# Softmax attention of three of four groups of sequences placed beside the first six units of a gated delta rule

## The chip, the cores and the metric

The kernel runs on one core of a Trainium2 chip, in 32-bit floats. The core's engines are TensorE (PE, matrix products; its weight loads are listed apart as PEld), VectorE (DVE), ScalarE (ACT), GpSimd (POOL) and SyncE (SP, which here only issues DMA transfers). Each engine works through its own instructions in order, and semaphores make it wait for others. A scheduler below the program decides the final order of each engine from the order in which the program issues its steps and from what depends on what.

The metric is the device time of one execution in microseconds (us). Where a time of the kernel is given it is the median of several executions; the profile is of one execution.

## The reference

Sixteen sequences of 128 tokens, 256 wide, pass through two residual blocks:

```python
x = x + delta_rule(attention(x, cond, Wq, Wk, Wv, Wo), W_qkv, W_z, W_b, W_a, conv_w, dt_bias, A_log, norm_w, W_out)
x = x + quantized_ffn(lora_ffn(x, ..., adapter_of_sequence), ...)
```

The attention is causal softmax attention with 16 heads of 16, its queries scaled by `min(precision, 4)` of the sequence; its result h feeds the delta rule:

```python
mixed = silu(causal_conv(h @ W_qkv, conv_w))        # 4 taps; 16 q and k heads, 32 v heads, 128 wide
q, k, v = split(mixed)
beta = sigmoid(h @ W_b)
g = -exp(A_log) * softplus(h @ W_a + dt_bias)
core = chunk_gated_delta_rule(l2norm(q), l2norm(k), v, g, beta)   # chunks of 64
core = core * rsqrt(mean(core * core) + 1e-6) * norm_w * silu(h @ W_z)
return core @ W_out
```

In the chunked rule g is summed along each chunk, its differences give a decay matrix, and a triangular system of 64 by 64 is solved for every head and chunk. The second block is a feed-forward network with an adapter per sequence, and a second one with weights rounded to 8-bit floats.

## The kernel before

The sequences are in four groups of four (`NG`, `GS`); a group has 512 tokens (`GT`). Four stages follow each other.

**1. Attention** (L119 to about L320, in pools `w1`, `p1` and its own three PSUM pools `ps_a`, `ps_s`, `ps_t`). `project(g)` makes queries, keys and values of a group; keys are copied twice (`ke`), each with the heads of one parity set to zero. The loop over n has NB + 2 slots; in a slot three sequences are worked on, at different steps: `scores(n)` (products `ps_sc` at L200, scale and mask into `sc` on DVE at L206, maximum at L212 on DVE, subtraction at L215 on POOL), `soften(n-1)` (exp on ACT at L229, sum at L234 and reciprocal at L235 on DVE, multiplication at L238 on POOL) and `weigh(n-2)` (transposes `ps_pt` L253 and copies, product with values `ps_o` L262, and a pick of the right head of each pair on ACT and DVE, L267 and L268). Each list has hand-written times that put the steps of a slot into one order. After four sequences `output(g)` multiplies by Wo and gives h of the group (`hT`, `ps_h` at L280) and the products for the gates (`ps_ba`).

**2. Gates**, `gates()` at L384, once for all sixteen sequences, when attention is done: `logs` (sigmoid, softplus by abs, exp and ln, on ACT and DVE), `rows` (sums along the chunk, stored in DRAM as `sums`) and `offsets`. SP then loads the sums of two units at a time, broadcast over partitions, into `aT` (`load_sums`, L427 on), and `fades` turns them into decay factors: a subtraction and a triangular select on POOL (L438, L439) and exp on ACT (L443).

**3. Units** of the delta rule, in pools `c2`, `w2`, `pc` and PSUM `ps_b` (six buffers) and `ps_r` (one, four accumulators of `ps_out`), which are opened after attention's have been closed. A unit is one key head with its two value heads for one group; there are 64. The loop `for n in range(N + LAST)` is a software pipeline with one slot for each unit, ordered by hand-written times between 0 and 24. In slot n:

- `keys` of unit n: products `ps_in` (L450), the first tap on ACT (L459), three taps on DVE (L461), silu (L478), squares (L482), norms (`ps_n`, L488; transposed on DVE, L490), factors on POOL (`nn`, L495, and `kn`, `c`);
- `decays` of unit n-1: weighting on POOL, products `ps_kq` (L525) and their scaling on DVE (L529), and DMAs that collect diagonal blocks (`diag`);
- for four units at a time (`NU`), `inverse`: 32 by 32 triangular inverses, mostly on DVE (products at L573), in two slots (units 0 to 3: slots 5 and 6), ending with `Tc` and `Uc`;
- `mergers` of unit n-7 (`MERGE`): DMAs that place `Uc` and `Tc` into the tiles `W` and `T`, and products that make 64 by 64 inverses of them. The first product is `ps_lo` at L664, in slot 7;
- `values` of unit n-7 (with weights `w_v`), `outputs` of unit n-8 (`w_gate`, `ps_z`, `ps_y`, `ps_ot`, norm) and `finish_unit` of unit n-10 (transposes `ps_zt`, `zT`, `ps_out` at L795, after the last head of a group the addition of x at L800 and the store of `x1`).

**4. Feed-forward networks**, in pools `w3` and `p3`, opened when the units' pools are closed. SP loads `acc` (all of x1, one transfer a group, L898), the adapter numbers and the weights, among them `gq`, `uq` and `dq`; `quantize` (L923 to L930) rounds these on DVE and POOL. PE transposes `acc` (`ps_xt`, L951), makes the adapter's small products (`lg`, `lu`, masked on DVE) and then `ps_gu` (L965), of which DVE makes `hid` (L974).

Of the kernel before, what the change touches and what calls it, by code (L numbers as in the profile page):

```python
# [53 lines left out]
def tile_adaln_attn_ffn(  # L54
# [16 lines left out]

    def filled(shape, value, name):
        t = const.tile(shape, F32, name=name, tag=name)
        G.memset(t, value)
        return t
# [3 lines left out]

    tri = pa.tile([P, P], F32, name="tri", tag="gm")  # L80
    G.memset(tri, 1.0)
    G.affine_select(out=tri, in_=tri, pattern=[[1, P]], compare_op=ALU.is_ge,
                    fill=0.0, base=0, channel_multiplier=-1)
    G.memset(tri[HALVES[0], HALVES[1]], 0.0)
    tri_2 = pa.tile([P, P], F32, name="tri_2", tag="gm2")
    G.tensor_copy(tri_2, tri)
    G.memset(tri_2[HALVES[0], HALVES[0]], -1.0)
    G.affine_select(out=tri_2[HALVES[0], HALVES[0]], in_=tri_2[HALVES[0], HALVES[0]], pattern=[[-1, C]],
                    compare_op=ALU.is_gt, fill=0.0, base=0, channel_multiplier=1)
# [6 lines left out]
    row = const.tile([P, 1], I32, name="row")  # L96
    G.iota(row, pattern=[[0, 1]], base=0, channel_multiplier=1)
    V.tensor_scalar(row, row, 4, 1, ALU.arith_shift_right, ALU.bitwise_and)
    odd = const.tile([P, 1], F32, name="odd")
    V.tensor_copy(odd, row)  # L100
    even = const.tile([P, 1], F32, name="even")
    V.tensor_scalar(even, odd, -1.0, 1.0, ALU.mult, ALU.add)
    parity = (even, odd)
# [7 lines left out]
    sums = dram.tile([NK * NB * 2, S], F32, name="sums")  # L111
# [3 lines left out]
    with ExitStack() as st:  # L115
        w1 = st.enter_context(tc.tile_pool(name="w1", bufs=1))
        p1 = st.enter_context(tc.tile_pool(name="p1", bufs=2))
        ps_a = st.enter_context(tc.tile_pool(name="ps_a", bufs=2, space=PSUM))
        ps_s = st.enter_context(tc.tile_pool(name="ps_s", bufs=4, space=PSUM))  # L119
        ps_t = st.enter_context(tc.tile_pool(name="ps_t", bufs=2, space=PSUM))  # L120

        xT_sb = w1.tile([P, ND, NT], F32, name="xT_sb")
# [9 lines left out]
        xTv = xT.rearrange("(c p) t -> p c t", p=P)  # L132
        for w, t in ((wqT, wq_sb), (wkT, wk_sb)):
            nc.sync.dma_start(out=t, in_=w.rearrange("(c p) e -> p c e", p=P))
        nc.sync.dma_start(out=xT_sb[:, :, 0:GT], in_=xTv[:, :, 0:GT])
        nc.sync.dma_start(out=wv_sb, in_=wvT.rearrange("(c p) e -> p c e", p=P))
        nc.scalar.dma_start(out=pr, in_=prec.rearrange("b o -> (b o)").partition_broadcast(P))
        nc.sync.dma_start(out=wo_sb, in_=woT.rearrange("(c p) e -> p c e", p=P))
        for g in range(1, NG):
            nc.sync.dma_start(out=xT_sb[:, :, g * GT : (g + 1) * GT], in_=xTv[:, :, g * GT : (g + 1) * GT])  # L140
# [6 lines left out]
        V.tensor_scalar(pr, pr, 4.0, 0.25, ALU.min, ALU.mult)  # L147

        grp = {}

        def project(g):
            d = grp[g] = {}
            qT = d["q"] = p1.tile([P, ND, GT], F32, name="qT", tag="qT")
            ke = d["k"] = p1.tile([P, ND, GS, 2, S], F32, name="ke", tag="ke")
            vt = d["v"] = p1.tile([P, GS, D], F32, name="vt", tag="vt")
            d["oT"] = p1.tile([P, ND, GT], F32, name="oT", tag="oT")

            def qk(w, e):
                ps = ps_a.tile([P, GT], F32, name="ps_qk", tag="a")
                for c in range(ND):  # L160
                    T.matmul(ps, lhsT=w[:, c, e * P : (e + 1) * P], rhs=xT_sb[:, c, g * GT : (g + 1) * GT],
                             start=c == 0, stop=c == ND - 1)
                if w is wq_sb:
                    A.copy(qT[:, e, :], ps)
                else:

                    for h in range(2):
                        A.activation(ke[:, e, :, h, :], ps.rearrange("p (s t) -> p s t", t=S), AF.Copy, scale=parity[h])

            def vproj(i):  # L170
                ps = ps_a.tile([P, 2, D], F32, name="ps_v", tag="a")
                for j in range(2):
                    t0 = g * GT + (2 * i + j) * S
                    for c in range(ND):
                        T.matmul(ps[:, j, :], lhsT=xT_sb[:, c, t0 : t0 + S], rhs=wv_sb[:, c, :],
                                 start=c == 0, stop=c == ND - 1)
                A.copy(vt[:, 2 * i : 2 * i + 2, :], ps)

            return (
                [lambda e=e: qk(wq_sb, e) for e in range(ND)]  # L180
                + [lambda e=e: qk(wk_sb, e) for e in range(ND)]
                + [lambda i=i: vproj(i) for i in range(GS // 2)]
            )

        HB = P // HD
        NPR = HB // 2
        seq = {}

        def scores(b):

            g, i = divmod(b, GS)
            d = seq[b] = {}
            cols = slice(i * S, (i + 1) * S)

            def product():

                d["ps"] = [ps_s.tile([P, ND, 2, S], F32, name="ps_sc", tag="s") for _ in range(NPR)]
                for e in range(ND):
                    for r in range(NPR):
                        T.matmul(d["ps"][r][:, e], lhsT=grp[g]["q"][BLOCKS[r], e, cols],  # L200
                                 rhs=grp[g]["k"][BLOCKS[r], e, i], start=True, stop=True)
                d["s"] = p1.tile([P, NPR, ND, 2, S], F32, name="sc", tag="sc", bufs=3)
                d["mx"] = p1.tile([P, 2, HB], F32, name="mx", tag="mx")

            def mask(r):
                V.scalar_tensor_tensor(out=d["s"][:, r].rearrange("p e h t -> p (e h) t"),  # L206
                                       in0=d["ps"][r].rearrange("p e h t -> p (e h) t"), scalar=pr[:, b : b + 1],
                                       in1=causal[:, None, :].to_broadcast([P, 2 * ND, S]),
                                       op0=ALU.mult, op1=ALU.add)

            def largest(n):
                V.tensor_reduce(out=d["mx"][:, n, :], in_=half(d, n), axis=AX.X, op=ALU.max)  # L212

            def less(n):
                G.tensor_tensor(half(d, n), half(d, n), d["mx"][:, n, :][:, :, None].to_broadcast([P, HB, S]),  # L215
                                ALU.subtract)

            return ([product] + [lambda r=r: mask(r) for r in range(NPR)]
                    + [lambda n=n, f=f: f(n) for n in range(2) for f in (largest, less)])

        def half(d, n):
            return d["s"][:, 2 * n : 2 * n + 2].rearrange("p r e h t -> p (r e h) t")

        def soften(b):

            d = seq[b]

            def exp(n):
                A.activation(half(d, n), half(d, n), AF.Exp)  # L229

            def total(n):
                if n == 0:
                    d["sm"] = p1.tile([P, 2, HB], F32, name="sm", tag="sm")
                V.tensor_reduce(out=d["sm"][:, n, :], in_=half(d, n), axis=AX.X, op=ALU.add)  # L234
                V.reciprocal(d["sm"][:, n, :], d["sm"][:, n, :])  # L235

            def share(n):
                G.tensor_tensor(half(d, n), half(d, n), d["sm"][:, n, :][:, :, None].to_broadcast([P, HB, S]), ALU.mult)  # L238

            return [lambda n=n, f=f: f(n) for n in range(2) for f in (exp, total, share)]  # L240

        def weigh(b):

            g, i = divmod(b, GS)
            d = seq[b]

            def turn(r):
                if r == 0:
                    d["pT"] = p1.tile([P, NPR, ND, 2, S], F32, name="pT", tag="pT")
                ps = ps_t.tile([P, ND, 2, S], F32, name="ps_pt", tag="t")  # L250
                for e in range(ND):
                    for h in range(2):
                        T.transpose(ps[:, e, h, :], d["s"][:, r, e, h, :], ident)  # L253
                A.copy(d["pT"][:, r], ps)

            def product(e):

                if e == 0:
                    d["po"] = ps_a.tile([P, ND, 2, S], F32, name="ps_o", tag="a")
                for r in range(NPR):  # L260
                    c0 = e * P + r * BL
                    T.matmul(d["po"][BLOCKS[r], e], lhsT=grp[g]["v"][:, i, c0 : c0 + BL],  # L262
                             rhs=d["pT"][:, r, e], start=True, stop=True)
# [9 lines left out]
        def output(g):  # L273
# [10 lines left out]
            def gates():  # L284
# [6 lines left out]
                if g > 1:  # L291
                    nc.sync.dma_start(out=h_dram[g], in_=hTs[g])
# [539 lines left out]
    for n in range(N + LAST):  # L832
# [47 lines left out]
        if n == N + 2:  # L880
            ffn_loads()
# [222 lines left out]
```

## Time and profile before

| what | us |
|---|---|
| time, median of 3 executions | 2496.53 |
| their range | 2491.33 to 2499.64 |
| the profiled execution's own time | 2490.03 |
| span of the profile (first to last instruction) | 2488.3 |
| first matrix product | 8.24 |
| first `ps_sc` | 21.84 |
| last `ps_o` of attention | 208.7 |
| first `ps_in` of unit 0 | 219.93 |
| first `ps_lo` (slot 7) | 354.79 |
| last `ps_out` of the units | 2059.55 |

The mean clock that TensorE was granted was 0.945 of full speed. All times below are from the start of the span. "Busy" is time in which an engine executes at least one instruction; a group's mean is that of one instruction, so that overlapping instructions (four `ps_sc` products run beside each other on different rows of the array) have a larger sum of means than busy time. The idle time at the end of a group's line is that of the engine just before these instructions, with the instruction whose end released it.

DMA issues that the text refers to, with KB of each and the median us from issue to landing:

```profile
aT<-sums SPq DMA_DIRECT2D x64, 512.0 KB, 5.3
w_qk<-in_w_qkv_dram SPq DMA_DIRECT2D x128, 128.0 KB, 2.3
w_v<-in_w_qkv_dram SPq DMA_DIRECT2D x64, 256.0 KB, 2.8
```

### The profile page before, as it was taken

Reading aid. Unit: us, or ns where it says so; the run is one execution under the profiler, and the core shown is the slowest. Engines: PE = TensorE matmul, PEld = TensorE weight load, DVE = VectorE, ACT = ScalarE, POOL = GpSimd, SP = SyncE. Lnnn points to the kernel's source line nnn. Section 1 sums busy time; section 2 is a strip of 40 time slices with the busy share of each in tenths; the row PEclk is TensorE's granted clock in tenths of the full one; section 3 lists DMA queues with packets and bytes.
Section 4 is the critical chain, followed back from the end, with each engine's and each line's share of the span. In section 5 each row is a group of like instructions: output and inputs, shape, how many; then the busy total and the mean of one; then the engine's idle time right before and its main releaser. Section 6 shows DMA issues by size and latency. Waiting matters only on the chain. (4 is left out here: it accounts for less than half of the span.)

```text
span 2488.3 us, 42071 instructions
## 1 busy us (share of the span) xinstructions
PE 2240.2 (90%) x16380; PEld 1488.2 (60%) x16380; DVE 1535.3 (62%) x2048; ACT 1330.4 (53%) x2954; POOL 1126.2 (45%) x813
## 2 busy tenths in 40 slices
PE   7996449899999899999989899999989997899999
PEld 4453226666676676666667676676767783344545
DVE  5663488687776968677696867769696522211111
ACT  4444326766666676766667676666766660011010
POOL 5664535465555646555564655456463224200000
PEclk9888679999999999999999999999999999999999
DMA  1004112222223322222332222233223213000000
GB/s 53 1 9 135 33 31 62 71 63 72 67 69 94 83 74 64 73 67 69 87 91 71 66 73 63 68 78 96 71 58 86 70 31 114 0 5 5 9 0 18
DMA packets 290533, 146.15 MB, mean 59 GB/s; under 512 B 183968, under 2 KB 279328, under 8 KB 290336
## 3 DMA queue, kind: packets, MB, share of 16 engines
q1 hardware_dynamic: 289904, 143.41, 21.7%
q8 instruction: 132, 2.16, 0.4%
q14 instruction: 65, 0.53, 0.1%
q10 hardware_dynamic: 432, 0.04, 0.0%
HBM read 116.91 MB, written 5.51 MB: 49 GB/s over the span
## 5 line engine op out<-in xcount | busy, mean ns | idle before, releaser
L461 DVE SCALAR_TENSOR_TENSOR cv<-ps_in,cw,cv 128x508 f32<-128x508 f32 (+2 forms) x768 | 539.7, 734 | 109.3 <-ACT cv L459 104.6
L459 ACT ACTIVATE cv<-ps_in,cw 128x512 f32<-128x512 f32 x256 | 174.4, 682 | 215.5 <-PE ps_in L450 214.1
L450 PE MATMUL ps_in<-hT,w_v 128*128 128x512 f32 x512 | 281.6, 678 | 5.8 <-DVE z L765 3.5
L450 PE MATMUL ps_in<-hT,w_qk 128*128 128x512 f32 x512 | 261.2, 635 | 11.2 <-DVE z L765 6.5
L765 DVE TENSOR_TENSOR z<-ps_ot,z 128x512 f32<-128x512 f32 x128 | 87.8, 686 | 290.1 <-ACT sq L763 290.1
L738 PE MATMUL ps_z<-w_gate,hT 128*128 128x256 f32 x1024 | 242.3, 379 | 0.8 <-DVE z L765 0.8
L795 PE MATMUL ps_out<-wo_head,zT 128*128 128x256 f32 x1024 | 239.6, 386 | 1.8 <-ACT zT L787 1.0
L495 POOL TENSOR_SCALAR nn<-turned 128x4 f32<-128x4 f32 x64 | 15.5, 242 | 469.2 <-DVE turned L490 342.0
L795 PEld LDWEIGHTS ps_out<-wo_head,zT 128*128 128x128 f32 x1024 | 188.7, 190 | 39.1 <-issue 12.0
L738 PEld LDWEIGHTS ps_z<-w_gate,hT 128*128 128x128 f32 x1024 | 189.5, 190 | 26.8 <-DVE z L765 1.7
L450 PEld LDWEIGHTS ps_in<-hT,w_v 128*128 128x128 f32 x512 | 102.9, 213 | 112.1 <-issue 105.4
L1026 POOL TENSOR_TENSOR o<-o,acc 128x512 f32<-128x512 f32 x8 | 10.1, 1264 | 337.0 <-DVE o L1025 337.0
L478 ACT ACTIVATE kq<-cv 128x512 f32<-128x512 f32 x128 | 80.1, 626 | 153.2 <-DVE cv L461 153.1
L763 ACT ACTIVATE sq<-ps_ot 128x128 f32<-128x128 f32 x512 | 143.2, 280 | 31.7 <-PE ps_ot L757 23.1
L525 PEld LDWEIGHTS ps_kq<-kq 128*128 128x128 f32 x512 | 104.6, 205 | 82.6 <-issue 63.0
L450 PEld LDWEIGHTS ps_in<-hT,w_qk 128*128 128x128 f32 x512 | 97.9, 202 | 93.0 <-issue 77.1
L751 ACT COPY y<-ps_y 128x512 f32<-128x512 f32 x128 | 75.0, 586 | 136.2 <-PE ps_y L750 135.0
L772 POOL TENSOR_TENSOR z<-z,r 128x1024 f32<-128x1024 f32 x64 | 131.7, 2058 | 24.7 <-DVE z L765 22.0
L785 PE MATMUL ps_zt<-ident,z 128*128 128x128 f32 x512 | 87.9, 298 | 58.0 <-DVE aT L529 56.7
L525 PE MATMUL ps_kq<-kq 128*128 128x256 f32 x512 | 136.4, 390 | 0.0
L757 PE MATMUL ps_ot<-y,aT 128*128 128x128 f32 x1024 | 135.3, 275 | 0.0
L750 PEld LDWEIGHTS ps_y<-v,W 128*128 128x128 f32 x1024 | 123.2, 193 | 16.5 <-ACT W L696 10.6
(203 smaller groups left out, 5009.9 us busy)
## 6 DMA issues: line engine op xcount, KB each, us to landing
aT<-sums SPq DMA_DIRECT2D x64, 512.0 KB, 5.3
w_qk<-in_w_qkv_dram SPq DMA_DIRECT2D x128, 128.0 KB, 2.3
w_v<-in_w_qkv_dram SPq DMA_DIRECT2D x64, 256.0 KB, 2.8
w_gate<-in_w_z_dram SPq DMA_DIRECT2D x64, 256.0 KB, 2.8
wo_head<-in_w_out_dram SPq DMA_DIRECT2D x64, 256.0 KB, 2.7
diag<-bT SPq DMA_DIRECT2D x256, 32.0 KB, 1.9
W<-Uc SPq DMA_DIRECT2D x256, 32.0 KB, 2.0
T<-Tc SPq DMA_DIRECT2D x128, 32.0 KB, 2.0
```

Source lines behind the costliest of these rows:

```text
L450: T.matmul(ps, lhsT=w[:, c, blk, :], rhs=hTs[g][:, c, :], start=c == 0, stop=c == ND - 1)
L459: A.activation(cv, psv, AF.Copy, scale=cw[:, col, 3:4])
L461: V.scalar_tensor_tensor(out=cv[:, :, sh:], in0=psv[:, :, : S - sh], scalar=cw[:, col, 3 - sh : 4 - sh], in1=cv[:, :, sh:], op0=ALU.mult, ...
L525: T.matmul(ps[:, j, :, :], lhsT=d["kq"][:, s, 0, :], rhs=d["kq"][:, s, :, :], start=True, stop=True)
L738: T.matmul(ps[:, j, :], lhsT=hTs[g][:, c, t0 : t0 + S], rhs=w_gate[u][:, c, :], start=c == 0, stop=c == ND - 1)
L750: T.matmul(ps[:, j, :], lhsT=d["W"][:, p, :], rhs=v[:, p, :], start=True, stop=True)
L757: T.matmul(ps[:, j, :], lhsT=d["aT"][:, p, :], rhs=d["y"][:, p, :], start=True, stop=True)
L763: A.activation(sq, ps[:, j, :], AF.Square, accum_out=d["r"][:, p : p + 1])
L765: V.tensor_tensor(z, ps, z, ALU.mult)
L772: G.tensor_tensor(d["z"], d["z"], d["r"][:, :, None].to_broadcast([P, NP, S]), ALU.mult)
L785: T.transpose(ps[:, j, :], d["z"][:, 4 * n + j, :], ident)
L795: T.matmul(ps[:, 2 * n + j, :], lhsT=d["zT", n][:, 2 * j + h, :], rhs=w_o[u][:, h, :], start=kh == j == h == 0, stop=kh == NK - 1 and j == ...
```

## The change

The pools of the early part of a unit (`c2`, `w2`, `pc`, and both PSUM pools) are opened before attention's, and attention's are opened above them; so both can be in use at the same time. Attention has no PSUM of its own: it takes tiles of the `ps_b` ring and, for `ps_o`, of `ps_r`, which now has two buffers of half the size (`ps_out` is one tile per half n). Some of attention's tiles take the place of tiles that the units use later (`qT` in `Uc`'s, `vt` in `Tc`'s). What the late part of a unit needs (`W`, `T`, `w_v`, `w_gate`, `wo_head`, `Mi`, `M2`, `v`, `z`, `y`, `r`, `sq`, `zT`, `x_in`) lies in pools of their own, opened in slot 7 by `open_late`, when attention's have been closed; the first `w_v` is loaded then.

`attention()` no longer runs a loop: it returns a list of steps with times, in units of a block. A block is half a sequence (8 heads): two score products of 64 rows and 512 columns, against keys that are copied four times, each with three of four heads set to zero (`fourth`), two masks, one maximum, one subtraction, and so on to one pick of half the width. The steps with times under `ALONE` = 11.2 run before the loop over units (group 0 has 8 blocks); the others are dealt out at `PACE` = 3.9 blocks a slot, in slots 0 to 6, in among the slot's own steps.

The gates are made for each group after its `output`: sigmoid as exp, addition of one and reciprocal; the absolute value on DVE; three products into one PSUM tile; and a DRAM tile of sums for each group. `load_sums(0)` is issued at time 5 of slot 0, and `fades(0)` takes the ordinary place of the other fades. The input `xT` is loaded by groups into two buffers, and its weights in another order.

```diff
+    st = ExitStack()
+    c2 = st.enter_context(tc.tile_pool(name="c2", bufs=1))
+    w2 = st.enter_context(tc.tile_pool(name="w2", bufs=2))
+    pc = st.enter_context(tc.tile_pool(name="pc", bufs=1))
+    ps_b = st.enter_context(tc.tile_pool(name="ps_b", bufs=6, space=PSUM))
+    ps_r = st.enter_context(tc.tile_pool(name="ps_r", bufs=2, space=PSUM))
...
+            def keys(e):
+                ps = product(wk_sb, e).rearrange("p (s t) -> p s t", t=S)
+                ke = d["k", e] = p1.tile([P, GS, 4, S], F32, name="ke", tag="ke")
+                for j in range(4):
+                    A.activation(ke[:, :, j, :], ps, AF.Copy, scale=fourth[:, j : j + 1])
...
+        def block(g, i, e):
...
+                d["ps"] = [ps_b.tile([P, 4, S], F32, name="ps_sc", tag="b") for _ in range(2)]
+                d["s"] = p1.tile([P, 2, 4, S], F32, name="sc", tag="sc", bufs=3)
+                for n in range(2):
+                    T.matmul(d["ps"][n], lhsT=grp[g]["q"][HALVES[n], e, cols], rhs=grp[g]["k", e][HALVES[n], i],
+                             start=True, stop=True)
...
+            return [product, lambda: mask(0), lambda: mask(1), largest, less, exp, total, share,
+                    lambda: turn(0), lambda: turn(1), weigh, pick]
...
+            def logs():
...
+                A.activation(e, ps[:, :, 0:NV], AF.Exp, scale=-1.0)
+                V.tensor_tensor(a, ps[:, :, NV:], dtb[:, None, :].to_broadcast([P, GS, NV]), ALU.add)
+                V.tensor_scalar(e, e, 1.0, None, ALU.add)
+                V.reciprocal(beta[:, :, g * GS : (g + 1) * GS, :].rearrange("p k b h -> p b k h"),
+                             e.rearrange("p b (k h) -> p b k h", h=2))
+                V.scalar_tensor_tensor(out=e, in0=a, scalar=-1.0, in1=a, op0=ALU.mult, op1=ALU.max)
+                A.activation(e, e, AF.Exp, scale=-1.0)
+                A.activation(e, e, AF.Ln, bias=one)
...
+        for g in range(NG):
+            t0 = GB * g
+            plan(t0, project(g), [-2, -1.8, -1, -0.8, -0.6, -0.4] if g == 0 else [-6.55, -5.55, -4.55, -3.55, -2.85, -1.85])
+            for i in range(GS):
+                for e in range(ND):
+                    plan(t0 + ND * i + e, block(g, i, e), [0, 0.15, 0.3, 0.45, 0.5, 1.0, 1.05, 1.45, 2.2, 2.45, 2.6, 2.8])
+            plan(t0 + GB, output(g), [2.15, 2.45, 3.0, 3.6])
+        return sorted(steps, key=lambda t: t[:2])
...
+    ALONE, PACE = 11.2, 3.9
     load_qk(units[0])
+    ahead = attention()
+    while ahead and ahead[0][0] < ALONE:
+        ahead.pop(0)[2]()
     for n in range(N + LAST):
...
+        now = [a for a in ahead if a[0] < ALONE + PACE * (n + 1)]
+        plan([f for _, _, f in now], [24 * ((t - ALONE) / PACE - n) for t, _, _ in now])
+        del ahead[: len(now)]
         if n == 0:
-            spread(gates() + [lambda: load_sums(0)] + [lambda i=i: fades(0)[i]() for i in range(3)])
+            plan([lambda: load_sums(0)], [5])
+        if n == MERGE:
+            st_1.close()
+            open_late()
+            load_v(at(MERGE))
...
-        if at(MERGE - 1):
+        if at(MERGE - 1) and n >= MERGE:
             load_v(at(MERGE - 1))
...
-        if n % 2 == 0 and 0 < n < N:
+        if n % 2 == 0 and n < N:
             plan(fades(n), [8, 12, 19])
...
+    late["stack"].close()
     st.close()
```

In the finished order POOL has the ten fades of the first five pairs of units among the subtractions and multiplications of the next five blocks after `ALONE`; SP has the `acc` loads of the feed-forward stage's first two groups ahead of the last two stores of `x1`, and DVE has the LoRA sums `lg` behind three operations of quantizing `gq`.

## The prediction

> **What bounds the kernel now.** I read the whole first, then the span in slices, then busy time by stage, then the waits of the stage that looks idle, last the timeline of the end. On the page:
>
> ```profile
> PE 2240.2 (90%) x16380; PEld 1488.2 (60%) x16380; DVE 1535.3 (62%) x2048; ACT 1330.4 (53%) x2954; POOL 1126.2 (45%) x813
> PE   7996449899999899999989899999989997899999
> DVE  5663488687776968677696867769696522211111
> ```
>
> TensorE (PE) is busy nine tenths of the span, except in slices 4 to 6 (each is 62.2 us). The change works there, so its worth is read there and not from the averages. Busy time by stretch (length; then PE, PE's loads, DVE, ACT, POOL, with instruction counts; then clock, DMA share, GB/s):
>
> ```profile
> 0.00:354.80 354.80, 246.08 (x1166) 129.04 (x1167) 210.74 (x291) 150.26 (x212) 192.94 (x145) 0.82 0.15 43
> 62.00:186.00 124.00, 114.51 (x619) 62.19 (x619) 84.32 (x117) 59.97 (x96) 79.38 (x43) 0.88 0.01 5
> 230.00:267.00 37.00, 13.81 (x40) 6.79 (x41) 9.00 (x15) 19.21 (x16) 32.60 (x25) 0.63 0.55 157
> 267.00:306.00 39.00, 18.63 (x57) 8.90 (x56) 20.32 (x32) 12.38 (x16) 13.38 (x16) 0.76 0.12 29
> 306.00:354.80 48.80, 17.77 (x58) 8.26 (x59) 44.90 (x53) 9.04 (x12) 19.97 (x15) 0.64 0.09 18
> 600.00:708.70 108.70, 101.69 (x897) 73.72 (x897) 81.97 (x110) 73.82 (x171) 59.80 (x44) 0.97 0.28 71
> ```
>
> The second line is attention alone: PE 92%, DVE 68%, POOL 64%. The next three are the first units of the delta rule, where nothing is 60% busy but POOL (88%) in the first, and DVE (92%, the inverse) in the last. The bottom line is four steady slots: 27.2 us each, PE 94%. The waits between 230 and 379 us (total, times, longest):
>
> ```profile
> PE ps_n L488 <- ACT sqa L482: 73.2, 8, 20.7
> POOL nn L495 <- DVE turned L490: 41.5, 5, 13.1
> ACT cv L459 <- PE ps_in L450: 39.5, 13, 4.9
> DVE cv L461 <- ACT cv L459: 34.0, 8, 7.9
> ```
>
> A unit's front is one chain over four engines (product, convolution, silu, square, norms, factors), with no other work beside it yet. So the 138 us from the last attention product (208.7) to the first merger product `ps_lo` (354.8; less some 8 us of output and gates) are latency. That hole is what attention's work is put into.
>
> **The work up to `ps_lo`.** From that product on, the instructions of every engine stand in the same order in both kernels, but for the tail and a few matmuls at group boundaries. Rows of the attention stage (count | busy, mean ns):
>
> ```profile
> L206 DVE SCALAR_TENSOR_TENSOR sc<-ps_sc,pr,causal 128x512 f32<-128x512 f32 x64 | 45.5, 733 | 30.2 <-PE ps_sc L200 30.2
> L234 DVE TENSOR_REDUCE sm<-sc 128x8 f32<-128x1024 f32 x32 | 39.0, 1218 | 29.9 <-ACT sc L229 29.8
> L215 POOL TENSOR_TENSOR sc<-sc,mx 128x1024 f32<-128x1024 f32 x32 | 60.6, 1896 | 53.1 <-DVE mx L212 44.4 <-DVE sm L235 7.1 <-PE ps_pt L253 0.9
> L268 DVE SCALAR_TENSOR_TENSOR oT<-ps_o,odd,oT 128x256 f32<-128x256 f32 x16 | 7.6, 476 | 11.5 <-ACT oT L267 11.5
> L200 PE MATMUL ps_sc<-ke,qT 32*128 32x256 f32 x256 | 44.5, 463 | 0.6 <-DVE sc L206 0.6
> L168 ACT ACTIVATE ke<-ps_qk,odd 128x512 f32<-128x512 f32 x8 | 5.4, 681 | 0.0
> L478 ACT ACT_TABLE_LOAD x4 | 5.1, 1283 | 4.3 <-DVE cv L461 4.2
> L438 POOL TENSOR_TENSOR aT<-aT,off 128x1024 f32<-128x1024 f32 x10 | 18.9, 1901 | 0.0
> ```
>
> *DVE.* Masks, maxima, sums and reciprocals keep number and size. Picks go from 16x476 ns = 7.6 to 32 of half the width, est. 340 ns (476 at 256 columns, 733 at about 508): 10.9, +3.3. Gates by group: four times nine operations of 128 columns at est. 290 ns = 10.4, for six of 512 at 0.69 = 4.1: +6.3. Small setup +0.6. 210.7 becomes 221.
>
> *ACT.* Four masked key copies per half in place of two: 16 x 0.68 = +10.9; picks +4.3. The units' silu now alternates with attention's exp, and the program has 25 table loads up to here for 11: 14 x 1.283 = +18.0. 150.3 becomes 184. **A rule against this:** the Trainium skill, "ScalarE: Activation LUTs", section "What ACT_TABLE_LOAD costs", prices a switch at the load plus 1.38 us of drain, about 2.66 us, and the next section asks for activations batched by set. This change unbatches them: 14 x 2.66 = +37, ACT 203. I take the row: the loads at L443 show 0.1 us idle ahead of them in three, those at L478 4.3 us in four, put down to DVE. On either count ACT stays below DVE, but each load stands in some chain.
>
> *PE.* Scores go from 256 instructions of 256 columns in four bands to 128 of 512 in two. Bounds: 30 us (128 x 0.47, the pace at which 512-column `ps_qk` follow each other, two beside each other) to 60 (one by one). The row's 44.5 is the middle, so I take no change, within 15. PE stays at about 246.
>
> *POOL.* 64 of attention's 1.9 us and ten fades (1.90 + 1.09) stay: 193. The W and T memsets (2.9 us) move to slot 7.
>
> **Attention alone.** In the middle stage 22 maxima (half sequences) take 124 us; all 32 take 187 (21.8 to 208.7): 5.85 us each. A block of the new loop is half a sequence with the same DVE work (2 x .733 + 1.21 + 1.22 + .20 + .34 = 4.4), POOL 3.8, PE 173/32 = 5.4. I keep 5.85. Start 22 (the first loads are only reordered, within 2); 11.2 blocks x 5.85 = 65.5. Slot 0 at about 88.
>
> **Merged stage.** DVE has done about 52 by then; 169 are left. PE: 246 - 14 - 11.2 x 5.4 = 172 left. POOL about 150. POOL's order puts all ten fades (30 us) among the next five blocks (10 x 1.9 = 19) and the factors and weights of units 0 and 1 (about 9), and the first waits behind group 0's gates and two DMAs (2.2 and 5.3 us by the issue table): about 58 to 64 us with POOL setting the pace and attention's subtractions queued behind fades. In them DVE does some 40. The other 126 of DVE, with PE near 90%, I run at 87%, between the 75% of the steady loop and the 92% of the inverse: 145. Together 209, so `ps_lo` at **297** instead of 354.8. I add 3 for the inverse, whose DVE operations take longer beside POOL (the 512-column product at L573 is 1.08 us at best and 2.38 in these slots) and now have attention's POOL work beside them: 300.
>
> **Slot 7.** Opening the late pools waits for attention's last readers, then `w_v` (2.8 us on the queue; SP has it behind the last sums and the diagonals) and the memsets. In before `w_v` came ahead unseen. Bounds 0 (still ahead of the first value product) to 5; I take +1.
>
> **Middle.** Same order, PE 94%: 0. PSUM's accumulator in two tiles: 0, PE waits for neither.
>
> **Tail.**
>
> ```profile
> 2059.55 1.96 PE L795 MATMUL ps_out<-wo_head,zT 128*128 128x256 f32 x8 [0.88 <-DVE x_in L800]
> 2067.48 2.65 SPq L898 DMA_DIRECT2D acc<-x  x4
> 2071.66 1.94 PE L951 MATMUL ps_xt<-ident,acc 128*128 128x128 f32 x8 [10.15 <-DMA acc<-x]
> 2123.13 2.93 PE L965 MATMUL ps_gu<-x1T,wu 128*128 128x512 f32 x3 [8.87 <-DVE hid L974]
> ```
>
> SP issued the feed-forward's `acc` loads after the last x1 store, at 2067.5. With the late pools closed apart, two of them come before either store and wait only for the last `zT` (2057), so PE's first transpose may start at 2061.5 for 2071.7. But DVE now has the LoRA sums behind three operations of quantizing `gq`, which lands about 9.6 us after issue, and the next long wait (8.9 us at 2123, for `hid`, behind quantizing) stands on DVE and POOL. Followed through, PE resumes at about 2117 instead of 2123: -6, bounds +2 to -10.
>
> **Sum.** Profiled execution 2490.0 (span 2488.3 and 1.7 around it) - 55 + 1 - 6 = 2430. The median, 2496.5, is 6.5 above the profiled one, and runs scatter by 8; I put the median of the new kernel at **2430** to 2435, headline 2430. This case alone, with the bounds above: 2412 to 2450.
>
> **Rivals.**
> - *A, it packs tighter.* PE and DVE feed one another and the merged stage runs like the inverse, DVE at 92 to 93%: 169/0.93 = 182, `ps_lo` at 270, time 2400. For: three engines have work for one another. Against: POOL's fades first. 0.20.
> - *B, POOL's head of line.* The fades go ahead of attention's subtractions and each waits for a sums load: 30 us more, `ps_lo` at 330, 2462. For: 88% POOL between 230 and 267. Against: three score buffers let PE and DVE run ahead a little. 0.14.
> - *C, no overlap, the slower side.* Engines execute in order, so unit and attention steps block each other: the units keep their 138 us, and the 20.8 blocks left (x 5.85 = 122), the table loads (18) and gates by group (10) stand in series with them: 88 + 138 + 122 + 28 = 376, +21, with the tail 2506. For: four-engine chains on both sides, score and PSUM rings shared. Against: units' chains leave gaps of up to 20.7 us. It costs time from the point where `ps_lo` comes after 361 (before's landmark and the tail's 6), that is where DVE is busy under 62% of the merged stage (169 of 273); over the whole stretch before it is 59% (211 of 355). 0.10.
> - *D, no effect.* Overlap is gained and lost in equal parts, `ps_lo` near 350. 0.03.
>
> The forecast itself: 0.53. What a measurement tells from no change is 0.3%, 7.5 us. Chances: faster 0.86, no change 0.03, slower 0.11. The range from A's 2400 to just above B, 2398 to 2464, leaves out C and D and some of A's lower side.
>
> **What would show it.** Right: first unit product near 90, `ps_lo` near 300, DVE about 221 busy up to it, POOL over 85% for the 60 us after slot 0, 25 table loads, then the same distance from `ps_lo` to the last unit as before (about 1704), first `ps_xt` within 5 us of the last unit product. Wrong: blocks alone slower than 5.85 (PE's scores at 60), DVE under 70% in the merged stage, PE waiting in slot 7 for `w_v`, or a distance after `ps_lo` that differs by more than 5.

## The result and the profile after

The changed kernel takes 2471.56 us (median of 4 executions, 2466.78 to 2475.05), the kernel before beside it 2494.01 (2491.33 to 2499.64): a ratio of 0.9906, with a 95% interval of 0.988 to 0.9932. A second measurement later gave 2471.34 against 2495.53, 0.9901 (0.9884 to 0.9917). The forecast was 2430 with a range of 2398 to 2464: the sign is right, the size a little over a third of what was foretold.

The profiled execution took 2466.78 us, its span is 2465.1 for 2488.3. Three landmarks divide the 23.2 us between them. Each is the start of one matrix product (the last `ps_out` is at 2061.1 before; 2059.55 is the start of its group of eight); the stretches are differences.

| stretch, us | before | after | difference | forecast |
|---|---|---|---|---|
| start to first `ps_lo` | 354.8 | 333.4 | -21.4 | -55 |
| first `ps_lo` to last `ps_out` | 1706.3 | 1709.0 | +2.7 | +1 |
| last `ps_out` to the end | 427.2 | 422.7 | -4.5 | -6 |

So the miss lies in the first stretch. The page of the changed kernel, totals and slices of 61.6 us:

```profile
PE 2233.8 (91%) x16264; PEld 1479.0 (60%) x16264; DVE 1548.6 (63%) x2099; ACT 1357.5 (55%) x3004; POOL 1123.0 (46%) x813
PE   7868768999999899999989899998999996999999
DVE  4657888777686967768696877769686523111111
```

TensorE's hole in slices 4 to 6 is gone, but slices 2 to 6 (61.6 to 370 us) are filled to 8, 6, 8, 7 and 6 tenths only. Busy time by stretch, in the columns of before (length; PE, PE's loads, DVE, ACT, POOL; clock, DMA share, GB/s):

```profile
23.60:95.90 72.30, 60.59 (x269) 29.23 (x269) 48.17 (x71) 34.43 (x58) 41.38 (x22) 0.88 0.05 15
95.90:160.00 64.10, 42.26 (x184) 20.00 (x183) 37.12 (x57) 42.15 (x56) 54.06 (x36) 0.84 0.27 94
160.00:297.00 137.00, 110.04 (x514) 53.29 (x514) 105.78 (x171) 81.33 (x121) 77.63 (x55) 0.91 0.07 17
297.00:333.40 36.40, 13.38 (x58) 7.83 (x55) 32.99 (x35) 12.63 (x16) 13.06 (x8) 0.72 0.09 26
0.00:333.40 333.40, 239.65 (x1050) 117.43 (x1051) 225.25 (x342) 178.43 (x262) 189.64 (x142) 0.88 0.13 40
600.00:708.70 108.70, 101.98 (x904) 73.87 (x896) 81.97 (x111) 73.88 (x171) 59.82 (x45) 0.97 0.27 71
```

The first row is attention alone (11.2 blocks in 72.3 us, 6.46 each), the second the 64 us that the prediction gave POOL as pacemaker (POOL is busy 84%), the third units and attention together, the fourth the inverse after attention's last product (296.8), with DVE at 91%. The totals in the fifth are close to the prediction's (DVE 225 for 221, ACT 178 for 184, PE 240 for 246, POOL 190 for 193). The steady slots in the last are as before. What is off is not the work but how fast it goes: between 160 and 297 us, the heart of the overlap, PE is busy 80%, DVE 77%, ACT 59%, POOL 57%. No engine is busy throughout. The waits between 95.9 and 333.4 us (total, times, longest):

```profile
POOL sc L241 <- DVE sm L238: 33.3, 8, 8.7
ACT sc L233 <- POOL sc L230: 29.3, 11, 8.5
PE ps_pt L248 <- POOL sc L241: 28.8, 8, 10.5
PE ps_sums L313 <- DVE gd L306: 26.5, 4, 20.0
POOL sc L230 <- DVE mx L227: 19.7, 8, 8.6
DVE bT L505 <- PE ps_kq L501: 18.6, 3, 14.2
```

Before, one long wait stood out (`ps_n` for the squares). Now they run in a ring through all four engines: maximum, subtraction, exp, sum, multiplication, transposes, each engine waiting for the one before it. Followed back from the first `ps_lo` by what released each instruction, the chain of the 237.5 us from 95.9 on spends 72 us on POOL, 63 on DVE, 59 on PE, 24 on ACT and 20 on nothing the profile shows. The prediction had made DVE its bound.

### The profile page after: what moved, and what is told of

It is laid out like the page before. It is cut to its first block, busy times and chain, and to the rows that moved or that the text cites. A ratio compares the mean times of both kernels' runs of the same rounds, so it can differ in the third digit from the quotient of the medians.

```text
span 2465.1 us, 41929 instructions
## 1 busy us (share of the span) xinstructions
PE 2233.8 (91%) x16264; PEld 1479.0 (60%) x16264; DVE 1548.6 (63%) x2099; ACT 1357.5 (55%) x3004; POOL 1123.0 (46%) x813
## 5 line engine op out<-in xcount | busy, mean ns | idle before, releaser
L426 PE MATMUL ps_in<-hT,w_qk 128*128 128x512 f32 x512 | 248.9, 608 | 4.7 <-DVE z L741 3.5
L761 PE MATMUL ps_zt<-ident,z 128*128 128x128 f32 x512 | 88.0, 298 | 59.9 <-DVE aT L505 57.7
L726 PEld LDWEIGHTS ps_y<-v,W 128*128 128x128 f32 x1024 | 123.5, 194 | 16.5 <-ACT W L672 10.6
```

What stands on the lines that cost most here:

```text
L426: T.matmul(ps, lhsT=w[:, c, blk, :], rhs=hTs[g][:, c, :], start=c == 0, stop=c == ND - 1)
L726: T.matmul(ps[:, j, :], lhsT=d["W"][:, p, :], rhs=v[:, p, :], start=True, stop=True)
L761: T.transpose(ps[:, j, :], d["z"][:, 4 * n + j, :], ident)
```

## The experiments

For each run, the first `ps_lo` of its profile is the reading; it was 333.4 in the changed kernel (the fastest of its four executions), and 340.6 in a second profile of the same kernel (the slowest of its four), at a lower granted clock; both are shown below. Most runs have one profile; a difference of less than some 8 us between two of them is not taken as shown, unless their granted clocks are alike.

**How much does the overlap hide?** All of attention ahead of the units:

```diff
-    ALONE, PACE = 11.2, 3.9
+    ALONE, PACE = 40, 3.9
```

> The changed kernel with all of attention ahead of the units (ALONE 40 for 11.2): new blocks and gates by group, but nothing of a unit beside attention except fades. If the overlap is worth what the prediction took it for, `ps_lo` comes 55 later than in the changed kernel, about 385 or more; if the overlap is worth little and the 21 us won come from elsewhere (gates and fades early), at 345 to 355. Attention alone: by the 6.5 us a block of the first stretch the last `ps_o` is at 232 plus the fades' 30.

`ps_lo` came at 383.8, so the overlap is worth 50 (43 against the second profile of the changed kernel, whose clock was nearer). Its stages:

```profile
22.70:259.00 236.30, 188.17 (x829) 91.08 (x828) 145.45 (x218) 120.70 (x190) 149.36 (x84) 0.82 0.09 30
110.00:150.00 40.00, 27.33 (x102) 11.74 (x94) 16.73 (x24) 22.13 (x29) 39.93 (x26) 0.62 0.16 63
270.90:383.80 112.90, 56.97 (x162) 26.36 (x161) 77.34 (x106) 27.11 (x36) 39.46 (x39) 0.71 0.16 40
```

The units' early part in series takes 112.9 (134.9 before, when the fades stood in it). Attention takes 236 for the 187 of before: the ten fades now lie in it (the second row: POOL 39.9 of 40), and so do the gates of three groups. The series sum is near rival C's 376; the prediction took 76 of it to be hidden, and 50 are. The overlap works, and hides at least a third less than forecast.

**Is it the depth of the buffers?** Five score buffers for three:

```diff
-                d["s"] = p1.tile([P, 2, 4, S], F32, name="sc", tag="sc", bufs=3)
+                d["s"] = p1.tile([P, 2, 4, S], F32, name="sc", tag="sc", bufs=5)
```

> The changed kernel with five score buffers `sc` for three (the input halves lie in the inverse's product tile to make room). First `ps_lo` was at 333.4 us against the 300 of the prediction. Theory 1, depth: three buffers now hold three half sequences where before's held three whole ones, so a block waits for the chain of the third before it; with five, `ps_lo` comes at 310 to 318. Theory 2 (POOL's hoisted fades) and theory 3 (table switches): the chain starts as late as before, `ps_lo` at 328 to 334. Theory 4 (TensorE, busy 85% between 160 and 240 us, is the limit): 330 to 334.

332.3. The order of instructions came out the same on every engine and the granted clock was 0.90, so this is a clean test: depth is not what holds the blocks.

**Fades spread, and no exp, with a new order each time.** A dependence of each pair's fades on the factors of the unit before, and `AF.Copy` for `AF.Exp`:

> The changed kernel with two tiny POOL operations that make the fades of unit n wait for the factors of unit n-1, so that eight of the ten fades can't run ahead of attention's subtractions. Theory 2: between 116 and 156 us only three blocks began, for seven at 5.6 us each; most of these 23 us come back, `ps_lo` at 313 to 320. Theories 1, 3, 4: the fades must be done some time, at most 5 us come back, `ps_lo` at 328 to 338.

> The changed kernel with a copy in place of attention's exp (the softmax is left out; the operation keeps its size), so that attention asks for no table: some 16 of 25 loads before `ps_lo` go. Theory 3, the loads stand in the chains: 16 x 1.28 = 20 us and more, `ps_lo` at 308 to 315. Theories 1, 2, 4: ACT is busy 57%, its loads are in its gaps: at most 8 us, `ps_lo` at 325 to 334.

345.5 and 349.9: both later than the changed kernel, the second with nine table loads fewer. In both the scheduler had put the instructions into another order, so neither tests its cost. Their granted clock between 96 and 230 us was low too (0.83 and 0.81); beside the second profile of the changed kernel, whose clock was 0.82, they are still 5 and 9 us late. The other order is what is left to explain that; it was not tried by itself.

**The same costs with the order held.** From here on the finished order of the changed kernel is pinned on each engine by a dependence of every instruction on the one ahead of it there:

```diff
     with tile.TileContext(nc) as tc:
         tile_adaln_attn_ffn(tc, *args)
+        in_order(tc, nc)
```

> Without exp again, but with the changed kernel's finished order of instructions pinned on every engine, so that only the table loads (16 of attention's and its neighbours' up to `ps_lo`) differ. Theory tables: they stand in the chains, `ps_lo` at 333 - 20 = 313 or earlier. Theory order (no single cost counts much; what counts is which instruction stands ahead of which): 322 to 333, and the 350 of the run without pinning was the scheduler's other order.

> Pinned order; the ten fades of the first five pairs work on an eighth of their columns (the rest of these decay factors is left out), some 26 us of POOL less between 105 and 156 us. Theory POOL's lump: `ps_lo` 18 to 26 earlier, 307 to 315. Theory order or TensorE: at most 10 earlier.

> Pinned order; maxima and sums of the softmax over 16 of 128 keys (the rest is left out of them), some 64 x 1.05 = 67 us of DVE less over all of attention. Theory DVE (the prediction's bound): the 21 blocks of the merged stage lose 2.1 us each, `ps_lo` 40 or more earlier, at 293 or less. Theory POOL or TensorE: 5 to 20 earlier.

> Pinned order; score products of 128 columns for 512 and value products of 128 for 256 (three of four score blocks and half of the value product are left out; all other operations keep number and size), some 50 us of TensorE less over all of attention, 17 of it ahead of slot 0. Shares of a removed microsecond that came back so far: fades (POOL) 14.7 of 26, maxima and sums (DVE) 25.5 of 67, table loads (ACT) none of 20. Theory TensorE (the real bound, behind DVE's 80%): more than two thirds come back, `ps_lo` at 300 or earlier. Theory coupling (no engine is the bound; each shares in the chains): 15 to 25 earlier, 308 to 318. Theory DVE or POOL: less than 10.

Slot 0 is taken from its first unit product:

| run | removed up to `ps_lo`, by its trace | slot 0 | `ps_lo` | slot 0 to `ps_lo` | granted clock, 96 to 230 us |
|---|---|---|---|---|---|
| changed kernel | | 95.9 | 333.4 | 237.5 | 0.91 |
| the same, second profile | | 96.0 | 340.6 | 244.6 | 0.82 |
| no exp | 9 of 25 table loads, 11.1 us of ACT | 94.4 | 337.1 | 242.8 | 0.87 |
| fades of an eighth | 22.9 us of POOL | 95.0 | 318.7 | 223.6 | 0.92 |
| short maxima and sums | 59.9 us of DVE | 85.1 | 307.9 | 222.8 | 0.91 |
| short score and value products | 23.5 us of PE | 90.9 | 327.7 | 236.8 | 0.84 |

The stretch from slot 0 to `ps_lo` in three of them (fades, maxima and sums, products; length, then PE, PE's loads, DVE, ACT, POOL), beside which the changed kernel has PE 165.7, DVE 175.9, ACT 136.1 and POOL 144.8:

```profile
95.04:318.68 223.64, 163.34 (x750) 80.30 (x749) 175.50 (x261) 135.86 (x191) 121.89 (x98) 0.88 0.14 42
85.07:307.85 222.78, 161.57 (x749) 78.79 (x748) 136.14 (x261) 135.18 (x192) 144.53 (x98) 0.87 0.13 42
90.94:327.70 236.76, 152.52 (x750) 87.97 (x748) 176.15 (x263) 136.13 (x193) 144.63 (x99) 0.80 0.13 39
```

(The removed amounts are differences of busy time; they are smaller than the expectations had them.) The runs of POOL and DVE have the clock of the first profile and are read against it. Of a microsecond of POOL 0.64 came back (14.7 of 22.9), of DVE 0.43 (25.5 of 59.9). From slot 0 on it is 13.9 of 22.9 for POOL, but only 14.7 of 39.8 for DVE, the prediction's bound: the rest of DVE's gain was made in attention alone. Both gains lie between what the rival theories expected. Table loads gave nothing back beyond the spread: 337.1, at a clock of 0.87, lies between the two profiles. For PE no share can be given, since the clock was lower in that run: against the first profile 5.7 of 23.5 came back, which is the range expected if DVE or POOL were the bound, against the second, with the nearer clock, 12.9.

So DVE was not the bound of the merged stage as a whole. Nor was any other single engine shown to be: a bound would give back nearly all of its own. The theory of coupling fits, but the place matters too. Between the first silu of unit 0 and that of unit 1 (105.4 and 149.8 in the changed kernel) the shorter fades gained 11 us and the shorter maxima and sums nothing (the gain on DVE stood at 11 at both), so POOL does pace that part, as the prediction had it; after it DVE's gain grew to 25.5. A bound that changes from stretch to stretch is a rival which these runs don't exclude.

**Other paces, order free.**

> The changed kernel with attention dealt out at 5 blocks a slot for 3.9 (slots 0 to 4 for 0 to 6); the scheduler orders anew. If the two streams share the engines' time freely, `ps_lo` stays within 5 of 333. If a slot costs its blocks plus what is left of the unit's own 13.8 us in series (the 36 us of slots 1 to 4 are 3.9 x 6.5 + 11), fewer slots pay: slots 0 to 4 take 43 each, slots 5 and 6 their own 23, the same 260 in sum from slot 0: `ps_lo` 330 to 345.

> 17 blocks ahead of slot 0 and 2.7 a slot beside the units (11.2 and 3.9 in the change). All alone gave 383.8, the change 333.4: 50 us for 20.8 blocks beside the units, 2.4 us a block. If every block beside the units hides that much, 15 give 36 and `ps_lo` is at 348. If only so much hides as the units leave idle, whatever the number of blocks, it stays at 330 to 338.

5 blocks a slot: 356.4, beyond both expectations; slots 0 to 4 took 58, 46, 44, 43 and 36 us (silu to silu). 17 blocks alone and 2.7 a slot: 338.2, within the spread of the changed kernel, though only 15 blocks lay beside the units. This fits the second expectation, that what is hidden depends on what the units leave idle and not on how many blocks are put there; with the order free, and granted clocks of 0.83 and 0.78, neither run shows it alone.

**The tail alone.** In the kernel before, the late tiles in pools that are closed first, nothing else:

```diff
+    late.close()
     st.close()
```

> The kernel before with nothing changed but that the late tiles of a unit lie in pools of their own, closed ahead of the others (as in the change). Theory of the prediction's tail: the acc loads are issued ahead of the last x1 stores and the stretch from the last ps_out to the end is 4 to 6 us shorter than before's 427.2, as in the changed kernel (422.7), with the rest within 2. Rival: the tail's gain comes with the other order of the whole, and stays away here: 426 to 428.

From the last `ps_out` to the end: 422.4 for 427.2, as in the changed kernel. The rest got 11 us longer (`ps_lo` 356.6, then 1715.3 for 1706.3), and the time was 2496.13, for 2495.97 of the kernel before beside it. The order was the same as before but for the loads of SP, where a load of `x_in` came early, and the tail itself. Two profiles of one order, the changed kernel (1709.0) and the gates in PSUM (1714.4, below), differ by 5 in this middle stretch; the rest of the 9 is not explained. So the first expectation's tail is right, its "rest within 2" is not, and no gain in the whole time was seen.

**The fades' place.** POOL between 116 and 158 us in the changed kernel (start, us):

```profile
118.38 1.90 POOL L230 TENSOR_TENSOR sc<-sc,mx 128x1024 f32<-128x1024 f32 x1
120.24 1.90 POOL L241 TENSOR_TENSOR sc<-sc,sm 128x1024 f32<-128x1024 f32 x1
...
128.35 2.15 POOL L415 TENSOR_SCALAR_AFFINE_SELECT aT<-aT 128x1024 f32<-128x1024 f32 x2
130.47 3.75 POOL L414 TENSOR_TENSOR aT<-aT,off 128x1024 f32<-128x1024 f32 x2
134.19 1.89 POOL L241 TENSOR_TENSOR sc<-sc,sm 128x1024 f32<-128x1024 f32 x1
...
143.71 3.76 POOL L414 TENSOR_TENSOR aT<-aT,off 128x1024 f32<-128x1024 f32 x2
147.42 2.13 POOL L415 TENSOR_SCALAR_AFFINE_SELECT aT<-aT 128x1024 f32<-128x1024 f32 x2
149.52 1.89 POOL L241 TENSOR_TENSOR sc<-sc,sm 128x1024 f32<-128x1024 f32 x1
```

Fades for units 2 to 9, which nobody needs before 200 us, stand ahead of softmax operations that everybody waits for: from 120.2 to 149.5 us only three multiplications (L241) begin, and between 125.9 and 155.8 no maximum does. In the next kernel they are moved, by hand, to later places in the pinned order, just ahead of need:

> Pinned order, all work done, but eight fades and their exp are moved by hand from the five blocks after slot 0 to later places in POOL's and ACT's order, each ahead of the weighting that needs it. Theory POOL's lump: blocks 13 to 16 come at 6 to 7 us each and `ps_lo` at 313 to 322. Theory order: what is won there is given back where the fades now stand, 328 to 340.

> The fades at later places alone, timed. If the gain of both (16 us, ratio 0.9844 against 0.9901) is a sum of like parts: 2461 to 2466, a ratio of 0.986 to 0.989. If the fades alone carry it: 2454 to 2458. If they do nothing and the first look was a matter of the granted clock: 2468 to 2474.

326.1 in the first run and 323.9 in the second, whose slot 0 came 2 earlier; the time is 2459.71 (2458.97 to 2462.36), a ratio of 0.9861 (0.9844 to 0.9877), 11.6 us under the changed kernel's 2471.34. Pure order, no work removed. Both expectations of the first run hold in part: from slot 0 on, the silu of unit 2 came 14 us earlier, `ps_lo` only 7, so half was given back where the fades now stand.

**The gates' operands.** Groups of the changed kernel up to 333.4 us:

```profile
L297 DVE TENSOR_SCALAR ea<-ea 128x128 f32<-128x128 f32 x4 | 6.5, 1637 | 0.0
L304 DVE SCALAR_TENSOR_TENSOR a<-a,ea 128x128 f32<-128x128 f32 x4 | 4.1, 1032 | 2.2 <-ACT ea L303 2.2
L298 DVE RECIPROCAL beta<-ea 128x128 f32<-128x128 f32 x4 | 3.8, 950 | 0.1
```

The first of these operations, of 128 columns, takes 1.64 us in the mean. The timeline of the last of them shows why (start, us):

```profile
314.05 5.46 POOL L549 TENSOR_TENSOR prod<-inv,gm 128x2048 f32<-128x2048 f32 x1 [11.60 <-DVE gm L596]
...
314.67 4.93 DVE L297 TENSOR_SCALAR ea<-ea 128x128 f32<-128x128 f32 x1
```

It ends at 319.60, POOL's operation at 319.51. Where POOL was idle, the same instruction took 0.22. The Trainium skill says so in "SBUF — State Buffer", section "Who interferes with whom": `tensor_scalar` can enter a mode that takes a pair of ports shared with GpSimd, an operation with two SBUF inputs needs one of them too, and the second comer is held until the first is done. This trace agrees: in two places L297 began 0.6 and 0.8 us after an operation of POOL and ended 0.08 us after it (4.93 and 1.19 us long); L304, with two sources in SBUF, took 2.01 and 1.54 us beside POOL and 0.29 without. The prediction had costed the gates without it. The edit gives both operations a source in PSUM:

```diff
-                A.activation(e, ps[:, :, 0:NV], AF.Exp, scale=-1.0)
+                A.activation(ps[:, :, 0:NV], ps[:, :, 0:NV], AF.Exp, scale=-1.0)
...
-                V.tensor_scalar(e, e, 1.0, None, ALU.add)
+                V.tensor_scalar(e, ps[:, :, 0:NV], 1.0, None, ALU.add)
```

(and the logarithm and L304 likewise).

> Pinned order, all work done; two operands of each group's gates (exp of -b, and the logarithm) lie in PSUM for SBUF, so that the DVE operations that read them have one SBUF source less and needn't wait for POOL's. In the changed kernel these eight operations took 6.5 + 4.1 us for some 2 when undisturbed. Theory chain (they lie on it with 10 us): `ps_lo` 6 to 9 us earlier, 324 to 328. Rival: PSUM makes no difference to what holds them, or the inverse beside the last of them is late anyway: 331 to 334.

> The gates' operands in PSUM alone, timed. Sum of like parts: 2461 to 2466. If they carry it alone: 2454 to 2458. If they do nothing: 2468 to 2474.

The two lines in the first of these runs, minimum, median and maximum in ns:

```profile
L297 DVE TENSOR_SCALAR ea<-ps_ba x4: 271/280/280, 92.0 to 310.2; 128x128 f32<-128x128 f32 x4
...
L304 DVE SCALAR_TENSOR_TENSOR a<-a,ps_ba x4: 271/287/289, 96.7 to 318.2; 128x128 f32<-128x128 f32 x4
```

None is held any more, though POOL was at work beside five of the eight. `ps_lo` at 326.8 and 326.2; the time is 2463.22 (2459.84 to 2464.78), ratio 0.9869 (0.9849 to 0.9888), 8.1 us under the changed kernel; the times of the two don't overlap, their ratios' intervals just do.

**Both, and the changed kernel again.**

> Both at once: gates from PSUM and the eight fades at later places (which alone gave 7.3 us). Theory chain: the two lie in different stretches and add up, `ps_lo` 13 to 16 earlier, 317 to 321, and a time 0.5 to 0.7% below the changed kernel's. Rival (slack of one is used up by the other): 322 to 326.

> The changed kernel itself once more, on the same chip and beside the same runs of the kernel before: a ratio of 0.988 to 0.993 as first measured, and the first `ps_lo` within 1 us of 333.4.

Both: 2455.29 us (2453.78 to 2459.07), ratio 0.9844 (0.983 to 0.9859), `ps_lo` at 321.8: 16 us under the changed kernel, somewhat less than the sum of 11.6 and 8.1; `ps_lo` lies just outside both expectations. This version beats both kernels. The second profile of the changed kernel gave the surprise: `ps_lo` at 340.6, and not within 1 us of 333.4. The same stretch in it, and in the first profile:

```profile
96.00:230.00 134.00, 106.25 (x435) 50.42 (x433) 84.24 (x129) 84.95 (x119) 89.84 (x61) 0.82 0.15 51
```

```profile
96.00:230.00 134.00, 104.03 (x470) 49.36 (x469) 90.24 (x138) 89.84 (x125) 95.20 (x67) 0.91 0.16 51
```

One program, one order, but a granted clock of 0.82 for 0.91, and 5 to 6 us less work of DVE, ACT and POOL done in the same 134 us. At the start of the stretch (the first silu of unit 0) the two are 0.1 us apart, at its end (that of unit 3) 7.6, and at `ps_lo` 7.2. The time went to PE: a `ps_in` product took 0.77 us in the mean for 0.64, and the chain back from `ps_lo`, followed as above, has 76 us on PE for 59, but 64 on POOL for 72.

## Why the prediction was wrong, by its steps

**Where it was right.** The hole of 138 us was latency, and attention's work fills it in part (all alone, 50 us more). The work by engine and the 25 table loads came as summed, PE's scores too (50.9 us for the 44.5 kept, within the 15 allowed). POOL did set the pace at the start of the merged stage; that this took the 64 us of the forecast was not measured apart, since the rows above are divided there. The steady slots didn't move. The tail's -4.5 is near the -6, but by another path (below).

**Attention alone, "I keep 5.85".** 6.46 a block: 72.3 us for 65.5, with 1.6 at the start, so slot 0 at 95.9 for 88. Inside a group most blocks come at 5.5 us (maximum to maximum); at the change of group at 8 to 10, where PE has output, gates and the next projection together. In the kernel before, the first twelve maxima, with a change of group among them too, span 53.8 us (25.1 to 78.9), here 69.5 (26.3 to 95.8): the new loop is slower over the same blocks, and not only in its change of group. Which step makes it so was not tried; five score buffers did not help (slot 0 at 94.9). +8.

**"The other 126 of DVE ... I run at 87%".** This is the step that failed: DVE as the bound of the rest of the merged stage. The rate was 80% (138.8 of 173.4), and DVE's work, made shorter, gave back 14.7 of 39.8 us from slot 0 on, where a bound would have given nearly all. The amount was off too. 169 less 40 is 129, a slip of 3, and in place of that 138.8 had to be done after 160 us: DVE had done 5.5 less by then (86.5 for 92), and its total was 225.3 for 221. The gates took 21.4 and not 10.4 (14.4 in the three lines above, seven more in 24 operations of 0.29), which other rows made up in part: the two 512-column products of the inverse for which 3 us were allowed took 1.05 each, for 2.38 before. In sum, as an estimate from these figures: amount (138.8 - 126)/0.87 = 15; rate 173.4 - 138.8/0.87 = 14; less the 3 allowed for the inverse: 25 or 26 us. With the 8 above this is the whole difference of 33 between 300 and 333.4. Choosing a rate between two rows (75% and 92%) was choosing a bound without asking which engine would give time back.

**Rivals.** B gave 2462 with `ps_lo` at 330 (2460 by the prediction's own sum), and the number is near, in part by luck: moved fades win 11.6 us in the whole time, not 33. A needed an engine that runs free, and none did. C's series sum (376 for 384) was good, and C is out: DVE was busy 74% of the merged stage (175.9 of 237.5), not under 62%. The prediction's own sign of being wrong, DVE under 70%, did not show either, so that share could not tell this outcome from the forecast; blocks slower than 5.85 did show.

**The rule weighed, table loads.** Row and rule differed by 19 us of ACT. The trace is with the row: ACT was busy 178 us for 184 and 203, and 21 of the 25 loads began 0.02 us after the instruction ahead of them, so that no drain shows ahead of them. With nine loads fewer and the order held, nothing came back beyond the spread.

**The tail, by its parts.** The first `ps_xt` was to come within 5 us of the last unit product; it comes 7.9 after, for 10.6 before:

```profile
2039.64 1.01 SPq L888 DMA_DIRECT2D acc<-x  x2
...
2045.88 0.37 SPq L393 DMA_DIRECT2D x_in<-in_x_dram  x1
...
2049.52 0.69 DVE L776 TENSOR_TENSOR x_in<-ps_out,x_in 128x512 f32<-128x512 f32 x1 [1.30 <-DMA x_in<-in_x_dram]
...
2050.27 1.11 PE L941 MATMUL ps_xt<-ident,acc 128*128 128x128 f32 x4 [7.50 <-DVE x_in L776]
```

And of the waits of SP between 2030 and 2060 us:

```profile
SPq L393 <- DMA x<-x_in: 2.4, 1, 2.4
```

The `acc` loads are early, as foretold (2039.6). But the tile `x_in` has one buffer: its last load stands behind them on SP and there waits for the store that empties it (2041.8) to land (2.4 us). It is issued 4.1 us after that store, for 2.1 before; why the store took longer was not tried. The last addition waits for this load, and PE's transposes for that addition, which by the program is the last reader of the units' PSUM. The prediction had named `acc` as the only wait. Of the 4.5 us, 2.7 were won up to the transposes and 1.8 behind them, for some 10 won and 4 lost in the forecast.

**Left open.** Why the granted clock differs between executions of one program, and so what PE's own share is. Whether the merged stage is held by a ring through all engines or by bounds that change along it. Why blocks alone take 6.46: the bunched PE work at the change of groups was read from the intervals, not tried.

## What to carry to other kernels

When two streams are put beside each other, sum the work by engine, but don't take the busiest engine for the bound without a run that shortens its work: here, with DVE and PE busy about 80% and chains through all engines, a microsecond saved came back at 0.64 on one engine and 0.43 on another, and the table loads of a third gave nothing that could be told from the spread. Look at the finished order for early-ready work with a late deadline that stands ahead of what everybody waits for. To test a cost where a scheduler orders anew, pin the order first: two runs without it told nothing of the cost they were made for. Read the granted clock of a profile before comparing single profiles.

## What was unexpected in the hardware

A 128-column DVE operation with one SBUF source took 0.22 us beside an idle POOL and 4.93 us beside a POOL product of 5.46; with its source in PSUM it took 0.27 to 0.28 in each of four places. And the granted clock of TensorE, 0.82 or 0.91 in the same stretch of the same program, came with a difference of 7.2 us, with PE busy 78% of it in the faster profile: half of what a stretch bound by PE would lose, by an estimate from the two clocks (134 x (0.91/0.82 - 1) = 14.7).
